# Per-graph products on 64 rows of the array, in a four-layer graph network on Trainium2

## The chip, the cores and the metric

The kernel runs on one core of a Trainium2 chip. TensorE multiplies matrices and writes PSUM, VectorE, ScalarE and GpSimd (POOL in the profile) do the elementwise work, and SyncE issues the DMAs. The metric is the device time of one execution in microseconds: 2607.68 us before, the median of four runs from 2606.7 to 2608.82.

## The reference

128 graphs of 64 nodes go through four layers; a node has 512 features. `adj` holds one 64 x 64 matrix per graph. All arithmetic is f32. Every layer first takes h = relu(layernorm(x)) and adds its result to x.

```python
# layer 0: hypergraph convolution, twice, with H = (adj != 0)
h = relu(hypergraph_conv(h, adj, W1, b1)); h = layer_norm(h, gamma, beta)
x = x + hypergraph_conv(h, adj, W2, b2) + h_in
# hypergraph_conv: D^-1 H B^-1 H^T (x W^T) + b, per graph
# layer 1: A = exp(lrelu(tanh(s_i + s_j))) * adj, normalised to P;  x = x + P h w
# layer 2: attention inside a graph, weight = adj * exp(q k^T), rows normalised
# layer 3: T = adj * exp(lrelu(s_i + s_j)), rows normalised
H = h Wk[0] + (T h) Wk[1] + (T T h) Wk[2] + biases;  x = x + relu(H)
```

Matrices that mix nodes (M = H B^-1 H^T of layer 0, P of layer 1, T and T² of layer 3) are 64 x 64 per graph. They are applied to h before the products with the weights.

## The kernel before

Two graphs share one tile of 128 rows (128 partitions), so x is 64 tiles of 128 x 512, worked on in 16 groups of four tiles. The mixing matrices of a tile's two graphs stand as a block-diagonal 128 x 128 matrix in a slot of the tag `bd`, whose off-diagonal blocks were set to zero once at the start; the two constants `HALVES` are the row ranges 0 to 63 and 64 to 127. Layers 0 and 1 are done for all groups, x goes out to DRAM and, after new weights have been loaded, layers 2 and 3 are done for all groups.

Products with weights use a Strassen scheme of seven products for a 2 x 2 block of tiles (`strassen`, `seven`; line 555 issues the matmuls, line 547 the sums on VectorE that it needs of its input). Ahead of them stand the products the change is about:

- `left_mul_T` computes (M h)^T in layer 0 and (P h)^T in layer 1 for a tile: four matmuls at line 502, each with 128 columns of h as weights and the block-diagonal matrix as 128 moving columns, into one PSUM bank; ScalarE copies the bank to SBUF at line 504, into a slot of `mT`. There are 128 such calls.
- In `layer3`, `tt` holds T^T and (T²)^T of a tile side by side, 256 columns. For each tile two operations `lm` at line 880 have two matmuls of 256 moving columns each, each operation with its own bank, and line 883 copies each bank into the tile's `a3`. Line 871 transposes h into the same `a3`.

The order of the instructions is neither the program's nor the hardware's choice. Every operation is recorded with an engine, an estimated cost, its reads and its writes (`pe`, `act`, `dve`, `pool`, `dma`); `Graph.run` then plans it all by list scheduling: on each engine the operation that could start first by these costs, ties by a priority that `step` moves on. A `Buf` gets a slot of its tag (a bank, for the tag `ps` with its eight banks) when its first operation is planned, and gives it back after its last. So a changed cost or a changed need for slots can move instructions on every queue, the DMA issues on SyncE's too. The cost of a group of matmuls is

```python
def c_mm(n, count):
    return 2 * count * max(n * 2 / 2400 + 0.0025, 0.111)
```

with n moving columns. Lines 413, 417 and 418 (`setup_l0`) are a few small matmuls near the start, the first with two columns of weights, the others with two rows.

Of the kernel before, what the change touches and what calls it, by code (L numbers as in the profile page):

```python
# [13 lines left out]
P = 128  # L14
C = 64
# [3 lines left out]
KD = D // P  # L19
# [19 lines left out]
class Graph:  # L39
# [41 lines left out]
    def run(self, slots, after):  # L81


        free = {tag: [(0.0, i) for i in range(len(ts))] for tag, ts in slots.items()}
        place = {}
        uses = dict.fromkeys(slots, 0)
        for o in self.ops:
            for b in o.bufs:
                uses[b.tag] += 1
        heirs = {}  # L90
        for tag, olds in after.items():
            for old in olds:
                heirs.setdefault(old, []).append(tag)
        waits = {tag: {old for old in olds if uses[old]} for tag, olds in after.items()}
        later = {tag: free[tag] for tag in after}
        for tag in after:
            free[tag] = []
        open_ = {e: [] for e in self.ENGINES}
        at = dict.fromkeys(self.ENGINES, 0.0)
        for o in self.ops:  # L100
            if not o.npre:
                open_[o.eng].append(o)
        order, left = [], len(self.ops)
        while left:
            best = None
            for e in self.ENGINES:

                t0, pick = None, None
                for o in open_[e]:
                    t = max(o.ready, at[e])  # L110
                    for b in o.bufs:
                        if id(b) not in place:
                            f = free[b.tag]
                            t = max(t, min(f)[0]) if f else float("inf")
                    if t0 is None or (t, o.prio, o.seq) < (t0, pick.prio, pick.seq):
                        t0, pick = t, o
                if pick is not None and (best is None or (t0, pick.prio) < (best[0], best[1].prio)):
                    best = t0, pick
            assert best and best[0] < float("inf"), "no operation can go on: too few slots"
            t, o = best  # L120
            open_[o.eng].remove(o)
            for b in o.bufs:
                if id(b) not in place:
                    s = min(free[b.tag])
                    free[b.tag].remove(s)
                    place[id(b)] = s[1]
                    b.t = slots[b.tag][s[1]]
            at[o.eng] = t + o.cost
            end = t + o.cost + self.LATENCY[o.eng]
            for b in o.bufs:  # L130
                b.users -= 1
                uses[b.tag] -= 1
                if not b.users:
                    free[b.tag].append((end, place[id(b)]))
                if not uses[b.tag]:
                    for tag in heirs.get(b.tag, ()):
                        waits[tag].discard(b.tag)
                        later[tag] = [(max(u, end), i) for u, i in later[tag]]
                        if not waits[tag]:
                            free[tag] = later[tag]  # L140
            for q in o.succ:
                q.npre -= 1
                q.ready = max(q.ready, end if q.eng != o.eng else t + o.cost)
                if not q.npre:
                    open_[q.eng].append(q)
            order.append((t, o.seq, o))
            left -= 1
        order.sort(key=lambda x: x[:2])
        for _, _, o in order:
            o.fn()  # L150
        return max(at.values()), {e: sum(o.cost for o in self.ops if o.eng == e) for e in self.ENGINES}
# [3 lines left out]
def tile_adj_preln_d4(  # L155
# [104 lines left out]
    def quad(b):  # L260
        return b.t.rearrange("p (c k) -> p c k", c=4)
# [233 lines left out]

    def left_mul_T(h, rhs, r, tag):

        p, m = Buf("ps"), Buf(tag)

        def mm():  # L500
            for c in range(KD):
                nc.tensor.matmul(quad(p)[:, c, :], h.t[:, c * P:(c + 1) * P], rhs(), start=True, stop=True)  # L502
        pe(c_mm(128, KD), mm, [h, *r], [p])
        act(0.59, lambda: nc.scalar.copy(m.t, quad(p)), [p], [m])  # L504
        return m

    def proj(lhsT, rhs, p, r, first=True, last=True):
# [110 lines left out]
    def layer0(g):  # L618
# [27 lines left out]
        for t0 in (0, 2):  # L646
# [12 lines left out]
            def emit_z(i, j, p, u, v, t0=t0, zs=zs):  # L659
# [1 line left out]
                scaled(lambda: z.t[:, cols], (z, j), lambda: rd.t[:, t:t + 1], [rd], lambda: b1_b[j].t, [b1_b[j]], p, u, v, D)  # L661
                act(0.63, lambda: nc.scalar.activation(z.t[:, cols], z.t[:, cols], AF.Relu), [(z, j)], [(z, j)])

            strassen(lambda i, j, mh=mh: mh[i].t[:, 2 * j:2 * j + 2, :], {(i, j): [mh[i]] for i in range(2) for j in range(2)},
                     W1, 2, D, "s1", emit_z)
            for i in range(2):
                z, rT = zs[i], rTs[i]
# [24 lines left out]
    def layer1(g):  # L692
        ad = adjs[g]
        hs, sg = [], Buf("col")
        for t in range(T):
            h = pre_ln(g, t)
            dot(lambda h=h: h.t, lambda: wa_b.t, lambda t=t: sg.t[:, t:t + 1], [h, wa_b], [(sg, t)])
            hs.append(h)
        z = bcast_sum(lambda: sg.t, lambda: sg.t, [(sg, t) for t in range(T)])
        act(0.42, lambda: nc.scalar.activation(z.t, z.t, AF.Tanh, scale=0.125), [z], [z])  # L700
        lrelu(z, 0.1)
        act(0.42, lambda: nc.scalar.activation(z.t, z.t, AF.Exp, scale=8.0), [z], [z])

        PT, pd, rn = Buf("bd"), Buf("ps"), Buf("ee")
        dve(0.42, lambda: nc.vector.tensor_mul(z.t, z.t, ad.t[:, 1]), [z, ad], [z])

        def sums():
            for i, m in enumerate((lambda: z.t, lambda: ad.t[:, 1])):
                nc.tensor.matmul(pd.t[:, i * T * C:(i + 1) * T * C], ones_bd, m().rearrange("p t c -> p (t c)"), start=True, stop=True)  # L709
        pe(c_mm(256, 2), sums, [z, ad], [pd])  # L710
        half = lambda i: pd.t[:, i * T * C:(i + 1) * T * C].rearrange("p (t c) -> p t c", t=T)
        dve(2.0, lambda: nc.vector.reciprocal(rn.t, half(0)), [pd], [rn])
        dve(0.42, lambda: nc.vector.tensor_mul(rn.t, rn.t, half(1)), [pd, rn], [rn])
        for s in HALVES:
            dve(0.42, lambda s=s: nc.vector.tensor_mul(PT.t[s, :, s], z.t[s], rn.t[s]), [z, rn], [(PT, s.start)])
        PTk = [(PT, 0), (PT, C)]
        step(1.0)
        for t0 in (0, 2):
            ph = [left_mul_T(hs[t], lambda t=t: PT.t[:, t, :], PTk, "mT") for t in (t0, t0 + 1)]
            step(1.8)  # L720

            def emit_w(i, j, p, u, v, t0=t0):
                xx, cols = xt[g, t0 + i], slice(j * D // 2, (j + 1) * D // 2)
                if u is not None:
                    U, iu = u
                    pool(0.75, lambda: nc.gpsimd.tensor_add(xx.t[:, cols], xx.t[:, cols], U.t[:, iu]), [xx, u], [xx])  # L726
                dve(c_v(D // 2), lambda: nc.vector.tensor_add(xx.t[:, cols], p.t[:, :D // 2], xx.t[:, cols]), [p, xx], [xx])

            strassen(lambda i, j, ph=ph: ph[i].t[:, 2 * j:2 * j + 2, :], {(i, j): [ph[i]] for i in range(2) for j in range(2)},
                     W, 2, D // 2, "s1", emit_w)  # L730
            for t in (t0, t0 + 1):
                xx = xt[g, t]
                xmid[g, t] = dram.tile([P, D], F32, name=f"xm{g}_{t}")
                dma(256, lambda xx=xx, t=t: nc.sync.dma_start(xmid[g, t], xx.t), [xx], [("xmid", g, t)])
# [96 lines left out]
    def layer3(g):  # L831
# [33 lines left out]
        for t0 in (0, 2):  # L865
            for t in (t0, t0 + 1):
# [4 lines left out]
                        nc.tensor.transpose(quad(p)[:, c, :], h.t[:, c * P:(c + 1) * P], ident)  # L871
                pe(KD * TR, tr0, [h], [p])
                act(0.59, lambda p=p, b=b: nc.scalar.copy(b.t[:, :KD, :], quad(p)), [p], [(b, 0)])
                for q in range(2):
                    pq = Buf("ps")

                    def lm(h=h, pq=pq, t=t, q=q):
                        for c in range(2):
                            cc = 2 * q + c
                            nc.tensor.matmul(pq.t[:, c * 2 * P:(c + 1) * 2 * P], h.t[:, cc * P:(cc + 1) * P],  # L880
                                             tt.t[:, t].rearrange("p j k -> p (j k)"), start=True, stop=True)
                    pe(c_mm(256, 2), lm, [h, (tt, 0), (tt, 1)], [pq])
                    act(0.59, lambda pq=pq, b=b, q=q: nc.scalar.copy(
                        b.t[:, KD:, :].rearrange("p (j c) k -> p c j k", j=2)[:, 2 * q:2 * q + 2],
                        pq.t.rearrange("p (c j k) -> p c j k", c=2, j=2)), [pq], [(b, 1 + q)])
                    step(0.9)
                step(0.45)

            def emit_o(i, j, p, u, v, t0=t0, os=[Buf("o"), Buf("o")]):
# [7 lines left out]
            ak = {}  # L897
            for i in range(2):
                b = a3[t0 + i]
                ak[i, 0] = [(b, 0), (b, 1)]  # L900
                ak[i, 1] = [(b, 1), (b, 2)]
            strassen(lambda i, j, t0=t0: a3[t0 + i].t[:, 6 * j:6 * j + 6, :], ak, W3, 6, D // 2, "s3", emit_o)

# [102 lines left out]
```

## Time and profile before

| | |
|---|---|
| profiled execution | 2606.7 us, span 2604.9 us |
| median of four runs | 2607.68 us |
| TensorE matmul | busy 2560.1 us, 12058 instructions |
| TensorE weight loads | busy 2046.2 us |
| VectorE | busy 1771.4 us |
| ScalarE | busy 783.2 us |
| GpSimd | busy 710.8 us |
| line 502 (M h, P h) | 1024 matmul records, all before 1320 us |
| line 880 (T, T²) | 512 matmul records, all after 1320 us |
| TensorE clock granted | 0.996 on average |

A matmul of f32 operands is two weight loads (PEld) and two matmul records (PE). The profile's time of one record is from its start until its results are out, and records overlap, so busy times of PE say little of how much more it could do; the step from record to record says more. Line numbers are those of the kernel before; in the kernel after, line 502 is 507, line 880 is 886 and line 555 is 561.

### The profile page before, as it was taken

Reading aid. Unit: us, or ns where it says so; the run is one execution under the profiler, and the core shown is the slowest. Engines: PE = TensorE matmul, PEld = TensorE weight load, DVE = VectorE, ACT = ScalarE, POOL = GpSimd, SP = SyncE. Lnnn points to the kernel's source line nnn. Section 1 sums busy time; section 2 is a strip of 40 time slices with the busy share of each in tenths; the row PEclk is TensorE's granted clock in tenths of the full one; section 3 lists DMA queues with packets and bytes.
Section 4 is the critical chain, followed back from the end, with each engine's and each line's share of the span. In section 5 each row is a group of like instructions: output and inputs, shape, how many; then the busy total and the mean of one; then the engine's idle time right before and its main releaser. Section 6 shows DMA issues by size and latency. Waiting matters only on the chain.

```text
span 2604.9 us, 32072 instructions
## 1 busy us (share of the span) xinstructions
PE 2560.1 (98%) x12058; PEld 2046.2 (79%) x12058; DVE 1771.4 (68%) x4064; ACT 783.2 (30%) x1370; POOL 710.8 (27%) x843
## 2 busy tenths in 40 slices
PE   8999999999999999999879999999999999999999
PEld 4767777777777777767768888888888888888887
DVE  8887788788787888778675545556456564555653
ACT  2343333343333433433222212222122221222211
POOL 3322334333233433333211212122221122211220
PEclk9999999999999999999989999999999999999999
DMA  4031001111001111101120110100101000010000
GB/s 166 17 110 37 20 22 37 33 37 37 21 21 37 33 37 37 37 10 32 65 89 21 33 33 25 37 25 29 33 24 37 29 29 33 21 37 25 25 21 25
DMA packets 53355, 96.18 MB, mean 37 GB/s; under 512 B 7760, under 2 KB 7760, under 8 KB 53200
## 3 DMA queue, kind: packets, MB, share of 16 engines
q1 hardware_dynamic: 53200, 94.14, 11.1%
q8 instruction: 94, 1.54, 0.3%
q14 instruction: 61, 0.50, 0.1%
HBM read 59.52 MB, written 34.60 MB: 36 GB/s over the span
## 4 chain that ended last, share of the span: by engine, by line
PE 95%; DVE 4%; issue 0%; ACT 0%; POOL 0%; DVEq 0%; ACTq 0%; POOLq 0%
PE ps L555 58%; PE ps L773 15%; PE ps L880 4%; PE ps L502 4%; PE ps L826 2%; PE ps L796 2%; PE ps L687 2%; PE ps L675 2%; PE ps L745 1%; PE ps L871 1%; DVE st L482 1%; DVE s_s_vu_tt L547 1%; PE ps L861 1%; PE ps L709 1%; PE ps L446 1%; PE ps L592 1%
## 5 line engine op out<-in xcount | busy, mean ns | idle before, releaser
L555 PE MATMUL ps<-wb_mem,rT_a 128*128 128x256 f32 x2056 | 476.2, 379 | 1.4 <-DVE u L527 0.8
L485 POOL TENSOR_TENSOR rs<-ve,mhalf 128x1 f32<-128x1 f32 x320 | 208.1, 653 | 935.7 <-DVE ve L484 874.0
L555 PEld LDWEIGHTS ps<-wb_mem,rT_a 128*128 128x128 f32 x2056 | 385.5, 190 | 67.2 <-issue 11.2
L493 ACT ACTIVATE h<-x,nm,rs 128x512 f32<-128x512 f32 x256 | 206.6, 815 | 360.3 <-DVE nm L492 270.9
L555 PE MATMUL ps<-wb_mem,s_s_vu_tt 128*128 128x256 f32 x1152 | 276.4, 379 | 0.1
L555 PE MATMUL ps<-wb_mem,tmp_s 128*128 128x256 f32 x1152 | 263.9, 379 | 0.0
L555 PEld LDWEIGHTS ps<-wb_mem,s_s_vu_tt 128*128 128x128 f32 x1152 | 215.6, 190 | 40.7 <-issue 7.3
L555 PE MATMUL ps<-wb_mem,mT_a 128*128 128x256 f32 x1016 | 243.3, 380 | 0.0
L555 PE MATMUL ps<-wa_mem,mT_a 128*128 128x512 f32 x512 | 240.1, 593 | 0.0
L555 PEld LDWEIGHTS ps<-wb_mem,tmp_s 128*128 128x128 f32 x1152 | 215.6, 190 | 27.5
L482 DVE BATCH_NORM_STATS2 st<-x 128x6 f32<-128x512 f32 x256 | 174.4, 686 | 63.4 <-DMA x<-xm 62.0
L555 PEld LDWEIGHTS ps<-wb_mem,mT_a 128*128 128x128 f32 x1016 | 190.5, 191 | 34.2 <-issue 7.7
L583 POOL TENSOR_TENSOR u<-u,bk_b 128x256 f32<-128x256 f32 x96 | 68.3, 726 | 472.0 <-DVE u L525 346.6
L555 PE MATMUL ps<-wa_mem,s_s_vu_tt 128*128 128x512 f32 x384 | 178.3, 594 | 5.5 <-DVE s_s_vu_tt L547 5.5
L527 DVE TENSOR_TENSOR u<-ps,u 128x512 f32<-128x512 f32 (+1 forms) x160 | 84.7, 529 | 115.6 <-PE ps L555 90.5
L555 PEld LDWEIGHTS ps<-wa_mem,mT_a 128*128 128x128 f32 x512 | 95.4, 190 | 85.7 <-issue 82.0
L502 PEld LDWEIGHTS ps<-bd,h 128*128 128x128 f32 x1024 | 131.1, 196 | 32.7 <-issue 18.7
L585 DVE TENSOR_TENSOR o<-ps,u 128x256 f32<-128x256 f32 x96 | 40.7, 424 | 153.5 <-PE ps L555 149.7
L504 ACT COPY mT_a<-ps 128x512 f32<-128x512 f32 x128 | 74.7, 584 | 233.6 <-PE ps L502 161.4
L726 POOL TENSOR_TENSOR x<-x,u 128x256 f32<-128x256 f32 x96 | 70.0, 742 | 260.8 <-DVE u L525 197.4
L502 PE MATMUL ps<-bd,h 128*128 128x128 f32 x1024 | 134.1, 280 | 6.9 <-ACT h L493 4.3
L555 PEld LDWEIGHTS ps<-wa_mem,s_s_vu_tt 128*128 128x128 f32 x384 | 71.9, 190 | 86.1 <-issue 68.6
(185 smaller groups left out, 4302.1 us busy)
## 6 DMA issues: line engine op xcount, KB each, us to landing
x<-in_x_dram SPq DMA_DIRECT2D x64, 256.0 KB, 2.8
xm<-x SPq DMA_DIRECT2D x64, 256.0 KB, 2.0
x<-xm SPq DMA_DIRECT2D x64, 256.0 KB, 2.6
out_dram<-x SPq DMA_DIRECT2D x64, 256.0 KB, 2.0
adj<-in_adj_dram SPq DMA_DIRECT2D x32, 256.0 KB, 2.6
wb_mem<-in_Wk_dram SPq DMA_DIRECT2D x6, 512.0 KB, 7.6
wa_mem<-in_W1T_dram SPq DMA_DIRECT2D x2, 1024.0 KB, 7.7
wb_mem<-in_W2T_dram SPq DMA_DIRECT2D x4, 512.0 KB, 6.4
```

The costliest lines, as they stand in the source:

```text
L482: dve(0.69, lambda i=i: nc.vector.bn_stats(st.t[:, i, :], src(i)), [r[i]], [(st, i)])
L485: pool(0.57, lambda: nc.gpsimd.tensor_tensor(rs.t, ve.t, mhalf, ALU.pow), [ve], [rs])
L493: act(0.82, lambda: nc.scalar.activation(h.t, xx.t, AF.Relu, bias=nm.t, scale=rs.t), [xx, nm, rs], [h])
L502: nc.tensor.matmul(quad(p)[:, c, :], h.t[:, c * P:(c + 1) * P], rhs(), start=True, stop=True)
L504: act(0.59, lambda: nc.scalar.copy(m.t, quad(p)), [p], [m])
L527: dve(c_v(n), lambda: nc.vector.tensor_add(at(2)(), p4.t[:, :n], at(1)()), [p4, (U, 1)], [(U, 2)])
L555: nc.tensor.matmul(p.t[:, :n], lhs()[:, c, :], rhs(c), start=first and c == 0, stop=c == kc - 1, skip_group_check=True)
L583: pool(0.75, lambda: nc.gpsimd.tensor_add(U.t[:, iv], U.t[:, iu], row()[:, cols]), [u, krow], [v])
L675: nc.tensor.transpose(quad(pt)[:, c, :], z.t[:, j * D + c * P:j * D + (c + 1) * P], ident)
L726: pool(0.75, lambda: nc.gpsimd.tensor_add(xx.t[:, cols], xx.t[:, cols], U.t[:, iu]), [xx, u], [xx])
L773: nc.tensor.matmul(pair(p.t)[:, o, :], a, b, start=first and o == 0 and c == 0, stop=c == 1, skip_group_check=True)
L880: nc.tensor.matmul(pq.t[:, c * 2 * P:(c + 1) * 2 * P], h.t[:, cc * P:(cc + 1) * P], tt.t[:, t].rearrange("p j k -> p (j k)"), start=True, ...
```

## The change

Each of the two products is split by graph: one matmul takes the 64 rows of the first graph and its 64 x 64 block, another the 64 rows of the second. The two go by turns and write two PSUM banks, one per graph. In `left_mul_T` a matmul has 64 moving columns; a call has eight instead of four, and two ScalarE copies of 256 columns instead of one of 512. In `layer3`, the four matmuls of 256 columns of a tile become eight of 128, in one operation instead of two, with two copies of 512 columns as before, now by graph and not by column. The zero blocks are no longer multiplied. The planner learns to wait until as many slots of a tag are free as an operation needs, and the costs and the keys of reads and writes follow.

```diff
@@ Graph.run
+                    need = {}
                     for b in o.bufs:
                         if id(b) not in place:
-                            f = free[b.tag]
-                            t = max(t, min(f)[0]) if f else float("inf")
+                            need[b.tag] = need.get(b.tag, 0) + 1
+                    for tag, n in need.items():
+                        f = free[tag]
+                        t = max(t, (min(f) if n == 1 else sorted(f)[n - 1])[0] if len(f) >= n else float("inf"))
@@ left_mul_T
-        p, m = Buf("ps"), Buf(tag)
+        p, m = [Buf("ps"), Buf("ps")], Buf(tag)
         def mm():
             for c in range(KD):
-                nc.tensor.matmul(quad(p)[:, c, :], h.t[:, c * P:(c + 1) * P], rhs(), start=True, stop=True)
-        pe(c_mm(128, KD), mm, [h, *r], [p])
-        act(0.59, lambda: nc.scalar.copy(m.t, quad(p)), [p], [m])
+                for i, half in enumerate(HALVES):
+                    nc.tensor.matmul(p[i].t[:, c * C:(c + 1) * C], h.t[half, c * P:(c + 1) * P], rhs()[half, half], start=True, stop=True)
+        pe(c_mm(64, KD), mm, [h, *r], p)
+        for i, half in enumerate(HALVES):
+            act(0.38, lambda i=i, half=half: nc.scalar.copy(m.t[:, :, half], p[i].t[:, :KD * C].rearrange("p (c k) -> p c k", c=KD)), [p[i]], [(m, i)])
@@ layer0 and layer1, keys of the Strassen products' input
-            {(i, j): [mh[i]] for i in range(2) for j in range(2)}
+            {(i, j): [(mh[i], 0), (mh[i], 1)] for i in range(2) for j in range(2)}
@@ layer3
-                for q in range(2):
-                    pq = Buf("ps")
-                    def lm(h=h, pq=pq, t=t, q=q):
-                        for c in range(2):
-                            cc = 2 * q + c
-                            nc.tensor.matmul(pq.t[:, c * 2 * P:(c + 1) * 2 * P], h.t[:, cc * P:(cc + 1) * P],
-                                             tt.t[:, t].rearrange("p j k -> p (j k)"), start=True, stop=True)
-                    pe(c_mm(256, 2), lm, [h, (tt, 0), (tt, 1)], [pq])
-                    act(0.59, lambda pq=pq, b=b, q=q: nc.scalar.copy(
-                        b.t[:, KD:, :].rearrange("p (j c) k -> p c j k", j=2)[:, 2 * q:2 * q + 2],
-                        pq.t.rearrange("p (c j k) -> p c j k", c=2, j=2)), [pq], [(b, 1 + q)])
-                    step(0.9)
+                pq = [Buf("ps"), Buf("ps")]
+                def lm(h=h, pq=pq, t=t):
+                    for c in range(KD):
+                        for i, half in enumerate(HALVES):
+                            nc.tensor.matmul(quad(pq[i])[:, c, :], h.t[half, c * P:(c + 1) * P], tt.t[half, t, :, half],
+                                             start=True, stop=True)
+                pe(c_mm(128, KD), lm, [h, (tt, 0), (tt, 1)], pq)
+                for i, half in enumerate(HALVES):
+                    act(0.59, lambda pq=pq, b=b, i=i, half=half: nc.scalar.copy(
+                        b.t[:, KD:, half].rearrange("p (j c) k -> p c j k", j=2),
+                        pq[i].t.rearrange("p (c j k) -> p c j k", c=KD, j=2)), [pq[i]], [(b, 1 + i)])
+                step(0.9)
                 step(0.45)
...
-                ak[i, 0] = [(b, 0), (b, 1)]
+                ak[i, 0] = [(b, 0), (b, 1), (b, 2)]
```

More of the change, by code (lines that the diff above doesn't have):

```diff
@@ L662, in emit_z @@
                 act(0.63, lambda: nc.scalar.activation(z.t[:, cols], z.t[:, cols], AF.Relu), [(z, j)], [(z, j)])
-            strassen(lambda i, j, mh=mh: mh[i].t[:, 2 * j:2 * j + 2, :], {(i, j): [mh[i]] for i in range(2) for j in range(2)},
+            strassen(lambda i, j, mh=mh: mh[i].t[:, 2 * j:2 * j + 2, :], {(i, j): [(mh[i], 0), (mh[i], 1)] for i in range(2) for j in range(2)},
                      W1, 2, D, "s1", emit_z)
@@ L727, in emit_w @@
                 dve(c_v(D // 2), lambda: nc.vector.tensor_add(xx.t[:, cols], p.t[:, :D // 2], xx.t[:, cols]), [p, xx], [xx])
-            strassen(lambda i, j, ph=ph: ph[i].t[:, 2 * j:2 * j + 2, :], {(i, j): [ph[i]] for i in range(2) for j in range(2)},
+            strassen(lambda i, j, ph=ph: ph[i].t[:, 2 * j:2 * j + 2, :], {(i, j): [(ph[i], 0), (ph[i], 1)] for i in range(2) for j in range(2)},
                      W, 2, D // 2, "s1", emit_w)
```

## The prediction

> **What bounds the kernel now.** I read the page's busy times and its chain first, then the groups split by shape, then the timeline at the lines the change touches. The page:
>
> ```profile
> PE 2560.1 (98%) x12058; PEld 2046.2 (79%) x12058; DVE 1771.4 (68%) x4064; ACT 783.2 (30%) x1370; POOL 710.8 (27%) x843
> ...
> PE 95%; DVE 4%; issue 0%; ACT 0%; POOL 0%; DVEq 0%; ACTq 0%; POOLq 0%
> ```
>
> TensorE is the chain: what its instruction stream gets longer or shorter, the span does, unless another engine has no room. The groups by shape:
>
> ```profile
> L502 PE MATMUL ps<-bd,h 128*128 128x128 f32 x1024 | 134.1, 280 | 6.9 <-ACT h L493 4.3 <-DVE bd L715 2.4
> L504 ACT COPY mT_a<-ps 128x512 f32<-128x512 f32 x128 | 74.7, 584 | 233.6 <-PE ps L502 161.4 <-PE ps L555 58.7 <-DVE s_s_vu_tt L547 13.5
> L880 PE MATMUL ps<-s_s_vu_tt,h 128*128 128x256 f32 x512 | 120.5, 379 | 0.0
> L523 ACT COPY u<-ps 128x256 f32<-128x256 f32 x96 | 35.7, 372 | 103.4 <-PE ps L555 103.4
> ```
>
> Each f32 matmul of the program leaves two records, so line 502 has 512 matmuls (128 calls of four), line 880 has 256 (64 tiles of four). The mean of one (280, 379 ns) is a latency; what a stream costs is the step from record to record, which the timeline gives:
>
> ```profile
> 46.65 0.97 PEld L635 LDWEIGHTS ps<-mB,bd 128*128 128x128 f32 x8
> 1000.47 2.75 PEld L502 LDWEIGHTS ps<-bd,h 128*128 128x128 f32 x24 [0.58 <-DVE bd L715]
> 1513.08 3.62 PE L880 MATMUL ps<-s_s_vu_tt,h 128*128 128x256 f32 x16
> ```
>
> A line's length less one record's own, over the records but one: (2.75 - 0.19)/23 = 0.111 us at line 502 with 128 moving columns, (0.97 - 0.19)/7 = 0.111 at line 635 with 65. So at and below 128 columns the step doesn't follow the columns: a weight load of 128 columns sets it. At 256 columns the matmul sets it: (3.62 - 0.38)/15 = 0.216.
>
> The changed matmuls use 64 rows of the array. The trace has only four places where the part of the array in use changes: into and out of line 413 (two columns of weights) and lines 417 and 418 (two rows).
>
> ```profile
> 34.55 1.45 PE L555 MATMUL ps<-wa_mem,s_s_vu_tt 128*128 128x512 f32 x3
> 35.93 1.02 PE L413 MATMUL ps<-wb_mem,gsc 128*2 128x512 f32 x2
> ...
> 41.94 1.02 PE L413 MATMUL ps<-wb_mem,gsc 128*2 128x512 f32 x2
> 42.89 0.44 PE L675 MATMUL ps<-ident,z_hT 128*128 128x128 f32 x2
> ...
> 43.93 0.49 PE L675 MATMUL ps<-ident,z_hT 128*128 128x128 f32 x3
> 44.35 1.12 PE L417 MATMUL ps<-o,tmp_s 2*128 2x512 f32 x2
> ...
> 45.31 1.02 PE L418 MATMUL ps<-o,tmp_s 2*128 2x512 f32 x2
> 46.26 0.55 PE L675 MATMUL ps<-ident,z_hT 128*128 128x128 f32 x3
> ```
>
> Records of 512 columns step by 0.43. The last L413 began at 41.94 + 0.43 = 42.37, would let the next start at 42.80, and that starts at 42.89: 0.09 late. The other three come out at 0.09 too (35.84 to 35.93; 44.26 to 44.35, with transposes stepping 0.109; 46.17 to 46.26, where ScalarE's h also ends just then). At an ordinary border, L502 to L555, there is no such hole. Besides, the next load is not under way: the L417 pair takes 1.12 where 0.43 + 0.59 = 1.02 would do (0.10 more), the L675 pair 0.44 for 0.38 (0.06 more). One change of shape costs 0.15 to 0.19 us.
>
> **The change part by part.**
>
> *Products with T and T² (line 880 before).* Removed: per tile eight records at 0.216, 1.73 us, 110.6 over 64 tiles. Added: per tile eight matmuls, 16 records of 128 moving columns on 64 rows, two row groups by turns. If the groups work side by side, each has eight loads at 0.111: 0.89 per tile, a gain of 0.84 each, 53.7 in all. If no two loads overlap, 16 x 0.111 = 1.78, a loss of 0.05 each, 3 in all. No row shows two row groups at once; these are the ends. I take the first.
>
> *M h and P h (line 502 before).* Removed: eight records at 0.111, 0.89 per call, 114 over 128 calls. Added: 16 records of 64 columns. Line 635 says that fewer columns don't shorten the step, so side by side it is 0.89 again, gain 0; one at a time 1.78, a loss of 0.89 each, 114 in all. I take 0. In these groups nothing is to be won even at best.
>
> [...]
>
> *Borders between the shapes.* In the changed kernel's instruction order the 64-row matmuls stand in 122 unbroken runs: 88 in layers 0 and 1 (65 of one call, 6 of two, 17 of three), 34 in layer 3 (19 of one tile, 15 of three). A run pays 0.19 on entry (0.09 and 0.10, as at L417) and 0.15 to 0.19 on leaving; mostly an f32 product follows, whose load is like L417's, so 0.19: 0.38 x 122 = 46.4. [...] And in each run the second row group ends about one load after the first, since a matmul's two records stand together and its group's turn comes after: 0.11 x 122 = 13.4; ends 0 and 13.4.
>
> *ScalarE copies.* Line 504's one copy of 584 ns becomes two of 256 columns, nearest row L523 at 372: +0.16 a call, 20 us on an engine that is busy 783. Cost nothing: it hides in ScalarE's idle time, and what waits for it, the sums of line 547 on VectorE, waited 13.4 us for mT_a in the whole run. On the path each time, it would be 20. Line 883's two copies per tile keep their size, but the first starts only after the whole product, some 0.9 later at most; the sums of layer 3 now wait for all three pieces. VectorE is at 726 of 1295 us in the second half (windows view), so 0 there too; were each of the 64 tiles 0.9 late on the path, 58.
>
> *PSUM.* A call holds two of eight banks instead of one, for 0.37 longer. What TensorE now waits for a bank's readers is 1.4 us (L555 on VectorE's u). I take 0, with an upper end of 10.
>
> *The plan.* Costs and needs in the planner change, so every queue is reordered: SP's 324 rows become 326, POOL's 677 become 676, with the loads and the inputs of POOL's adds moved along. TensorE's waits in the list of waits add up to 40 us (9.9 for ScalarE's h at the turn to layer 2, 6.1 at the start). I take them unchanged; a plan may move them 10 either way.
>
> Sum: -53.7 + 46.4 + 13.4 = +6.1. The profiled execution took 2606.7, the median is 2607.7: **2613**.
>
> **Rivals.**
>
> *Shape changes are free (the other side).* Place: the 122 runs. Then -53.7 + 13.4 = -40: 2566. The sign turns at (53.7 - 13.4)/122 = 0.33 us per run, entry and exit together. [...] Against it: four of four show the 0.09, among them both directions.
>
> *Records go out strictly in order.* [...] If a row group's load may not pass the other group's waiting record, then per four records (two of one group, two of the other) only a matmul and the other group's first load overlap: three steps of 0.11 at 64 columns, 1.31 per call of M h, and four at 128, 1.78. That is 128 x 0.42 + 64 x 0.05 + 46.4 = +103: 2710. [...]
>
> *Loads one at a time.* 114 + 3 + 46.4 = +163: 2770. The same comes if a record can't follow another in under 0.056 us, the pace of line 635 (two records per 0.111): 32 records a call are 1.78. For it: the load's 0.111 is the rigid number of this trace. Against it: at 42.89 a load and its matmul start together, so records can follow faster.
>
> **How the numbers follow.** Side by side with paid borders 0.50: 2613, own range 2595 (exit 0.15, no trailing group) to 2630 (PSUM and plan against it). In order 0.22: 2710. One at a time 0.18: 2770. Free borders 0.10: 2566. Faster and slower count from 0.2%, about 5 us, which is what a measurement here can tell. Faster: 0.10 and a quarter of the first, 0.23; same: a quarter of the first, 0.12; slower the rest, 0.65. The range reaches from 2592 to 2780; it leaves out the free borders and a little above.
>
> **What would show it.** Right: records of line 507 and 886 starting in pairs, one per row group, 0.11 per pair; a hole of 0.09 before and after each run; line 886's stretch per tile near 1.0 and not 1.73; ScalarE at some 803; TensorE's waits near 40. Wrong on the side of loss: 16 steps of 0.11 per call, the first half of the span longer by over 100. Wrong on the side of gain: no holes. The forecast falls if the pairs overlap only in part, since the gain and the price of the borders nearly cancel.

## The result, and the profile after

The changed kernel takes 2610.55 us (median of 41 runs, 2608.8 to 2613.6) against 2606.91 before (61 runs, 2605.94 to 2608.87; the 2607.68 above was the median of four): ratio 1.0014, 95% interval 1.001 to 1.0018. That is 3.6 us slower, clear of the noise but inside the 0.2% that the prediction counts as no change, and it hides a loss and a gain of some 30 us each. The profiled execution took 2610.86 us (before: 2606.7) with a span of 2609.0.

The page after the change, its busy times and its chain:

```profile
PE 2557.4 (98%) x13594; PEld 2015.9 (77%) x13594; DVE 1790.3 (69%) x4064; ACT 790.3 (30%) x1498; POOL 707.6 (27%) x843
...
PE 94%; DVE 5%; ACT 1%; issue 1%; POOL 0%; DVEq 0%; ACTq 0%; POOLq 0%
```

TensorE is still the chain, with 1,536 matmul records more. The groups by shape that answer to lines 502, 504 and 880:

```profile
L507 PE MATMUL ps<-bd,h 64*128 64x64 f32 x2048 | 137.7, 280 | 6.2 <-ACT h L496 4.2 <-DVE bd L721 2.0
L510 ACT COPY mT_a<-ps 128x256 f32<-128x256 f32 x256 | 81.7, 374 | 193.5 <-PE ps L507 121.2 <-PE ps L561 62.7 <-DVE s_s_vu_tt L553 9.3
L886 PE MATMUL ps<-s_s_vu_tt,h 64*128 64x128 f32 x1024 | 66.8, 279 | 9.5 <-ACT s_s_vu_tt L869 9.5
```

The matmuls of M h and P h doubled in number and kept their busy time (134.1 before, 137.7 now); those of T and T² doubled too, and theirs fell from 120.5 to 66.8. The 9.5 us of idle time before line 886 is new: line 880 had 0.0. The timeline of the kernel after, first TensorE's matmuls at three calls of line 507 in a row, then its weight loads there, then one tile of line 886 in the same two views; the line at the head is of the kernel before, three calls of line 502:

```profile
1000.55 2.87 PE L502 MATMUL ps<-bd,h 128*128 128x128 f32 x24
...
1009.60 0.59 PE L693 MATMUL ps<-y_qT,bd 128*128 128x512 f32 x1
1010.12 2.90 PE L507 MATMUL ps<-bd,h 64*128 64x64 f32 x48
1013.38 0.70 PE L561 MATMUL ps<-wa_mem,mT_a 128*128 128x512 f32 x1 [0.36 <-ACT mT_a L510]
...
1010.12 2.76 PEld L507 LDWEIGHTS ps<-bd,h 64*128 64x128 f32 x48 [0.76 <-issue]
...
1590.56 1.16 PE L886 MATMUL ps<-s_s_vu_tt,h 64*128 64x128 f32 x16
1591.65 3.70 PE L832 MATMUL ps<-s_s_vu_tt,bd 128*128 128x512 f32 x8
...
1590.55 0.97 PEld L886 LDWEIGHTS ps<-s_s_vu_tt,h 64*128 64x128 f32 x16
```

Three calls of line 507 have 48 records in the 2.9 us that 24 records of line 502 took before. Two loads, one per row group, go out per step, and the two of a pair start 0.007 us apart (in 1,398 of the 1,536 pairs). From the first of 24 pairs to the last there are 23 steps, from the first of eight to the last there are seven: (2.76 - 0.19 - 0.007)/23 = 0.111 us a pair at line 507 and (0.97 - 0.19 - 0.007)/7 = 0.110 at line 886. A single record of line 880 took 0.216. So the step of a pair is that of one record on all 128 rows (0.111 at line 502), at 64 moving columns and at 128. And the hole at the border is there: the last record of L693 began at 1009.60, its 512 columns take 0.43, and the next starts at 1010.12 and not at 1010.03, 0.09 late, as at lines 413 and 417 before.

The list of TensorE's waits after:

```profile
PE ps L877 <- ACT h L496: 9.9, 1, 9.9
PE ps L886 <- ACT s_s_vu_tt L869: 9.5, 14, 0.7
PE ps L641 <- DVE mB L636: 6.1, 1, 6.1
PE ps L598 <- DVE dg L596: 4.5, 1, 4.5
PE ps L507 <- ACT h L496: 4.2, 3, 3.7
PE ps L561 <- ACT mT_a L510: 2.1, 6, 0.4
```

Two lines are new: 9.5 us for the copy of T² (14 times 0.7) and 2.1 for the two copies of mT, one of which stands in the timeline above. Another line shrank, TensorE's wait for the sums of VectorE, first before and then after:

```profile
PE ps L555 <- DVE s_s_vu_tt L547: 5.5, 7, 1.0
...
PE ps L561 <- DVE s_s_vu_tt L553: 0.8, 1, 0.8
```

All of TensorE's waits in the list come to 39.9 us before and 46.4 after.

The turn from the first two layers to the last two shows in the end of M h and P h: their last record ended at 1316.9 us before and ends at 1349.5 now, 32.6 later, while what follows it went from 1288.0 to 1259.5, 28.5 less.

### The profile page after: what moved, and what is told of

The parts are those of the page before. It is cut to its first block, busy times and chain, and to the rows that moved or that the text cites. A ratio compares the mean times of both kernels' runs of the same rounds, so it can differ in the third digit from the quotient of the medians.

```text
span 2609.0 us, 35323 instructions
## 1 busy us (share of the span) xinstructions
PE 2557.4 (98%) x13594; PEld 2015.9 (77%) x13594; DVE 1790.3 (69%) x4064; ACT 790.3 (30%) x1498; POOL 707.6 (27%) x843
## 4 chain that ended last, share of the span: by engine, by line
PE 94%; DVE 5%; ACT 1%; issue 1%; POOL 0%; DVEq 0%; ACTq 0%; POOLq 0%
PE ps L561 58%; PE ps L779 15%; PE ps L507 4%; PE ps L886 3%; PE ps L832 2%; PE ps L681 2%; PE ps L802 2%; PE ps L693 2%; PE ps L751 1%; PE ps L877 1%; DVE u L579 1%; DVE st L485 1%; PE ps L867 1%; PE ps L598 1%; PE ps L715 1%
## 5 line engine op out<-in xcount | busy, mean ns | idle before, releaser
L488 POOL TENSOR_TENSOR rs<-ve,mhalf 128x1 f32<-128x1 f32 x320 | 197.6, 620 | 1133.0 <-DVE ve L487 1120.0
L561 PE MATMUL ps<-wb_mem,s_s_vu_tt 128*128 128x256 f32 x1152 | 282.9, 384 | 0.9 <-DVE s_s_vu_tt L553 0.8
L507 PEld LDWEIGHTS ps<-bd,h 64*128 64x128 f32 x2048 | 124.9, 191 | 51.0 <-issue 24.9
L529 ACT COPY u<-ps 128x512 f32<-128x512 f32 (+1 forms) x160 | 73.3, 458 | 242.4 <-PE ps L561 141.8
L507 PE MATMUL ps<-bd,h 64*128 64x64 f32 x2048 | 137.7, 280 | 6.2 <-ACT h L496 4.2
L510 ACT COPY mT_a<-ps 128x256 f32<-128x256 f32 x256 | 81.7, 374 | 193.5 <-PE ps L507 121.2
L589 POOL TENSOR_TENSOR u<-u,bk_b 128x256 f32<-128x256 f32 x96 | 81.4, 867 | 207.5 <-DVE u L533 100.7
L668 ACT ACTIVATE z_hT<-z_hT 128x512 f32<-128x512 f32 x128 | 80.8, 633 | 179.3 <-DVE z_hT L581 177.2
```

Source lines behind the costliest of these rows:

```text
L488: pool(0.57, lambda: nc.gpsimd.tensor_tensor(rs.t, ve.t, mhalf, ALU.pow), [ve], [rs])
L507: nc.tensor.matmul(p[i].t[:, c * C:(c + 1) * C], h.t[half, c * P:(c + 1) * P], rhs()[half, half], start=True, stop=True)
L510: act(0.38, lambda i=i, half=half: nc.scalar.copy(m.t[:, :, half], p[i].t[:, :KD * C].rearrange("p (c k) -> p c k", c=KD)), [p[i]], [(m, i)])
L529: act(n / 1200 + 0.17, lambda: nc.scalar.copy(at(0)(), p1.t[:, :n]), [p1], [(U, 0)])
L561: nc.tensor.matmul(p.t[:, :n], lhs()[:, c, :], rhs(c), start=first and c == 0, stop=c == kc - 1, skip_group_check=True)
L589: pool(0.75, lambda: nc.gpsimd.tensor_add(U.t[:, iv], U.t[:, iu], row()[:, cols]), [u, krow], [v])
```

## The experiments

### Each half of the change alone

The first version takes over the change of `layer3` and leaves `left_mul_T`; the second the reverse.

The main lines of the first edit, shortened (the copies, the costs and the keys go back with them):

```diff
 # t_only: left_mul_T as before
-        for c in range(KD):
-            for i, half in enumerate(HALVES):
-                nc.tensor.matmul(p[i]..., h.t[half, ...], rhs()[half, half], ...)
+        for c in range(KD):
+            nc.tensor.matmul(quad(p)[:, c, :], h.t[:, c * P:(c + 1) * P], rhs(), start=True, stop=True)
 ...
 # mp_only: layer3 as before, two operations lm of two matmuls of 256 columns
```

> Only the products with T and T^2 are split by graph; M h and P h stay as before. Theory (row groups work side by side, every run of 64-row matmuls pays for its two borders): 34 runs in layer 3 instead of 122. Line by line from the timelines of the two kernels, the stretches of these products with their borders and the new wait for tt add up to 30 us less than before: 2577, ratio 0.988. Rival (the parts are each near zero, the small result hides no gain and no loss): 2604 to 2610. Rival (waits and the new plan ate the gain of layer 3): no better than 2600, and a longer list of TensorE's waits.

> Only M h and P h are split by graph; layer 3 stays as before. Theory: 88 runs in layers 0 and 1, each 0.34 us longer than the full-height call that it replaces, nothing won inside: 2607 + 30 to 32 = 2638, ratio 1.012. Rival (each part near zero): 2604 to 2610. Rival (ScalarE's second copy or the second bank is what costs): longer too, but with holes at line 561 for mT_a or for VectorE's u and none at the borders.

T and T² alone: 2577.4 us (4 runs), ratio 0.9887, interval 0.987 to 0.9903: 29 less than the 2606.5 beside it. M h and P h alone: 2641.1 (4 runs), ratio 1.0129, interval 1.0114 to 1.0144: 35 more. Expected were 2577 and 2638. The sum of the two, +5.5, is near the whole change's +3.6. So the near zero is a gain and a loss that cancel, and the rival of two parts near zero falls. In the first version the wait for tt stands as in the kernel after:

```profile
PE ps L883 <- ACT s_s_vu_tt L866: 9.4, 14, 0.7
```

In the second, the waits for mT come to 2.2 us, which leaves the greater part of the 35 to the borders: a run of a single call (there are 65) takes 1.24 us from the end of the work ahead to the start of the work behind, with the weight load behind it that nothing hides, and a single call on full height takes 0.90 (medians). The 0.34 between them times 88 runs is 30.

### The price of a border by itself

```diff
         def mm():
+            nc.tensor.matmul(quad(p)[:, 0, :C], h.t[:C, :P], rhs()[:C, :C], start=True, stop=True)   # extra64
+            nc.tensor.matmul(quad(p)[:, 0, :C], h.t[:, :P], rhs()[:, :C], start=True, stop=True)     # extra128
             for c in range(KD):
```

> The kernel before, with one more matmul at the head of each of the 128 calls for M h and P h: 64 rows, 128 columns of weights, 64 moving columns, its result overwritten by the call's own first matmul; the plan is the same as before. Theory (a change of shape costs 0.2 us each way): per call 0.20 + 0.11 + 0.05 + 0.20 = 0.56, in all +72: 2679. Rival (changes of shape are free): as the 128-row control, +28: 2635.

> The control: the same additional matmul on all 128 rows, so two more records and no change of shape. Both theories: 2 x 0.111 x 128 = +28: 2635. The difference to the 64-row version is the price of 128 pairs of borders: 43 us by the theory (0.34 each), 0 by the rival.

2673.6 us (3 runs) and 2630.0 (3 runs), ratios 1.0257 (1.024 to 1.0274) and 1.0094 (1.0077 to 1.0111). Both are some 5 us under what was expected, as the control's two records cost 23.5 us and not 28. The difference of the two is 43.6 us, 0.34 per pair of borders, where 43 was expected. The timelines of TensorE in the two, at one call each:

```profile
1033.44 1.02 PE L688 MATMUL ps<-y_qT,bd 128*128 128x512 f32 x2
1034.40 0.43 PE L501 MATMUL ps<-bd,h 64*128 64x64 f32 x2
1034.76 1.16 PE L503 MATMUL ps<-bd,h 128*128 128x128 f32 x8
```

```profile
1019.73 0.33 PE L501 MATMUL ps<-bd,h 128*128 128x64 f32 x2
1019.90 1.11 PE L503 MATMUL ps<-bd,h 128*128 128x128 f32 x8
```

From the start of the additional matmul to the start of the call proper it is 0.36 us with a change of shape and 0.17 without; ahead of the 64 rows another 0.09 goes (1033.44 + 2 x 0.43 = 1034.30, the start is 1034.40; unrounded 0.092), and the call's first weight load is no longer hidden (1.16 for 1.11). The rival of free borders falls.

### How far ahead the other row group may start

The same matmuls and the same plan, but in another order inside a product: four of the first graph and then four of the second; two and two; three, three, one and one. The kernel after takes turns of one.

```diff
-            for c in range(KD):
-                for i, half in enumerate(HALVES):
+            for i, half in enumerate(HALVES):          # by_graph
+                for c in range(KD):
+            for i, c in ((0, 0), (0, 1), (1, 0), (1, 1), (0, 2), (0, 3), (1, 2), (1, 3)):   # by_two
+            for i, c in ((0, 0), (0, 1), (0, 2), (1, 0), (1, 1), (1, 2), (0, 3), (1, 3)):   # by_three
```

> The kernel after, with the two loops inside each product swapped: all four matmuls of the first graph, then all four of the second, where they went by turns. Same matmuls, banks, borders and plan. Theory (records for another row group can start while earlier records of the first still wait, as far ahead as the hardware looks): if it looks at least 8 matmul records ahead, no change, 2608 to 2613. Rival (records go out strictly in order, and only neighbours overlap): the two graphs run one after the other, 1.78 instead of 0.89 a call, 192 x 0.85 = +163: 2774. In between: a look-ahead of a few records.

> The kernel after, with the matmuls of each product in turns of two (two of the first graph, two of the second, and so on: 4 records a turn). In the version graph by graph, the second graph's first load began when the fifth of eight records had begun, that is, with three matmul records of the first still waiting. Theory (up to three matmul records of a row group may wait without holding up what comes behind): with four records to a turn the second group starts at once, no change: 2609 to 2613. Rival (each turn of a group has to end before the other starts, or the overlap is a fixed share of a turn): half way to the version graph by graph, 2640 to 2650.

> As before in turns of three, then one of each (6 records, 6 records, 2, 2). Theory (three may wait): the second group starts when the third record of the first has begun, some 0.27 us late, once per call and not once per run, and later turns catch up in part: 192 x 0.2 to 0.27 = +38 to +52 at most, less where calls stand together and the lag is already there; 2630 to 2660. If it comes out at 2611, more than three may wait.

| matmul records to a turn | time, us | ratio (interval) | a run of a single call is longer by (line 507 / line 886), us |
|---|---|---|---|
| 2 (the kernel after) | 2610.6 | 1.0014 (1.001 to 1.0018) | 0 / 0 |
| 4 | 2617.2 | 1.0037 (1.0024 to 1.0051) | 0.05 / 0.10 |
| 6 | 2643.7 | 1.0139 (1.0119 to 1.0159) | 0.27 / 0.32 |
| 8 | 2686.4 | 1.0302 (1.0282 to 1.0322) | 0.49 / 0.55 |

A turn is what one row group issues before the other is up. The last column, the lag, compares a run of a single call, or tile, with that of the kernel after. Neither end came: with eight records to a turn the groups overlap in part. Three tiles of line 886 in a row show it, in this version and then in the kernel after:

```profile
1516.61 3.93 PE L886 MATMUL ps<-s_s_vu_tt,h 64*128 64x128 f32 x48
```

```profile
1545.98 2.99 PE L886 MATMUL ps<-s_s_vu_tt,h 64*128 64x128 f32 x48 [0.68 <-ACT s_s_vu_tt L869]
```

In the trace the first group's fifth matmul record begins at 1517.159, and the second group's first load at 1517.164: three records of the first group still wait then. All 19 runs of a single tile show the same, and in the version of six the second group's first load comes just after the third record of six has begun, again with three waiting. With four records to a turn, where three wait behind the first, the second group starts at once, 0.007 us after the first. That turn costs a lag of 0.05 to 0.10 even so: 2617.2 lies 4 us above the expected 2609 to 2613. From there each two records more to a turn cost 0.22 us, two steps. For six I had expected a lag in every call; it comes once per run (0.27 in the runs of one call and in those of three), so 122 x 0.27 = 33, and 33 were measured. So in these runs records did hold up what stood behind them, but only from the fourth that waited (0.27 to 0.55 us in turns of six and eight). And matmuls of one group passed those of the other: the second group's first record begins at 1517.165, the first group's last, which stands ahead of it in the program, at 1517.494. The version with eight has one more thing against it: its granted clock was 0.992 on average in the profiled execution and 0.991 in the other two, against 0.995 in the kernel after. The reason is not shown.

### The new wait for T²

The planner puts the products with T and T² right behind the one that makes T², and TensorE waits for ScalarE's copy. A greater estimated cost for that copy lets the planner put two transposes of h between them; what is computed stays.

```diff
-        act(0.59, lambda: nc.scalar.copy(tt.t[:, :, 1, :], quad(p2)), [p2], [(tt, 1)])
+        act(1.40, lambda: nc.scalar.copy(tt.t[:, :, 1, :], quad(p2)), [p2], [(tt, 1)])
```

> As the version with only T and T^2 by graph, but the planner is told 1.40 instead of 0.59 us for ScalarE's copy of T^2 (tt), so that in 15 of 16 groups two transposes of h (line 874, 2 x 0.44 us) come between the product that makes T^2 and the first product that uses it. Nothing is computed differently. Theory (the 9.4 us that TensorE waits at line 883 for that copy, 14 times 0.7, is a wait of the plan, with work at hand to fill it): 2577.4 - 9 = 2568, and the wait is gone from the list. Rival (the wait moves to another place, as ScalarE or a bank is late): 2575 to 2580, with a new line in the list of waits.

> The same planner cost in the kernel after. Theory: 2610.6 - 9 = 2601, ratio 0.998 to the kernel before, so that without this one wait the whole change would have come out a little faster. Rival: 2608 to 2612, nothing gained.

With T and T² alone: 2568.3 us (4 runs), ratio 0.9851, interval 0.9837 to 0.9864. With the whole change: 2601.2 (11 runs), ratio 0.9979, interval 0.997 to 0.9988. Both are 9 less than without the edit, and the wait is gone from the list (the first version):

```profile
PE ps L874 <- ACT h L496: 9.9, 1, 9.9
PE ps L638 <- DVE mB L633: 6.1, 1, 6.1
PE ps L558 <- DVE s_s_vu_tt L550: 5.5, 7, 1.0
PE ps L505 <- ACT h L496: 4.5, 3, 3.7
```

The first of the two is the fastest kernel here: 38 us under the kernel before.

## Why the prediction was right, point by point

The predicted 2613 us stand against 2610.6, and the case named likeliest, side by side with paid borders, is the one that holds. The gain and the price of the borders were right in their sizes. Two other terms, the trailing group and the waits, were wrong by some 12 us each, and it is luck that they offset each other. By its own measure of 5 us the prediction gave "slower" 0.65 and "same", where 3.6 us falls, 0.12.

- **Gain at T and T²: right.** Predicted 0.111 per step of two loads and 53.7 us in all; measured 0.110 to 0.112, so 64 x (1.73 - 8 x 0.111) = 54.
- **No gain at M h and P h: right.** 0.111 a pair, as a record before; the half alone shows a loss only.
- **Price of the borders: right in sum.** Predicted 0.19 each way, 46.4 in all. In M h a run pays 0.09 ahead of its first pair, 0.05 until its second pair (0.16 us instead of 0.11), 0.10 ahead of the work behind and 0.10 for the load there: 0.34, times 88 runs 30. The 34 runs of T and T² take 81.2 us; less 64 x 0.89 for their steps and 9.5 for the wait, 15 are left, 0.43 a run. Together 45.
- **The trailing group, 13.4: wrong.** I had taken a matmul's two records to keep the other group waiting for a step. The two groups' records start 0.007 apart: 0.9 in all, which the 45 hold. The orders of six and eight show that a lag of that kind comes only when more than three records wait.
- **Waits unchanged: wrong.** The plan brought 9.5 for the copy of T², and ScalarE's second copy of mT 2.1, 11.6 together. I had set the copies at nothing because VectorE hardly waited for mT; it was TensorE that came to wait, where three calls stand together (the line at 1013.38). The other waits became 5 us shorter, so that the list grew by 6.5, within the 10 that the prediction allowed the plan.
- **ScalarE's time: over-sized, without effect.** Predicted 20 us more, measured 7.1 (783.2 to 790.3): of two copies in a row, part overlaps, as 256 copies of 374 ns are busy for 81.7 us.
- **The clock** was left out of the sum. At the turn of the layers the trace has the clock at half for 20 us in the kernel before and for 27 in the kernel after. TensorE is idle there for 22 and for 18 us. The windows view over 160 us at that place, before and after (behind the window stand its length and TensorE's busy time; the clock is the third number from the end):

```profile
1240.00:1400.00 160.00, 138.23 (x669) 116.07 (x667) 97.02 (x205) 38.24 (x67) 34.46 (x43) 0.94 0.19 61
```

```profile
1270.00:1430.00 160.00, 141.76 (x746) 119.11 (x745) 97.33 (x211) 38.46 (x73) 35.77 (x45) 0.91 0.16 53
```

  Seven more at half are at most 3.4 us. How much of it they cost is not shown; the half with M h and P h alone has it (0.91), and the other has not (0.94). Single runs show that a thousandth of granted clock goes with some 2 us: the kernel before took 2606.5 us in 18 of the runs beside the experiments, with a clock of 0.996, and 2608.5 in 16 with 0.995 (medians); the kernel after took 2610.2 in 33 runs with 0.995 and 2612.4 in nine with 0.994. At 0.995 the two are 1.7 us apart.

The new sum is -54 + 45 + 11.6 = +3; measured +3.6 in the medians and +4.2 in the profiled executions. The timelines say the same without the terms. Line 886's 34 runs take 81.2 us, borders and waits included, where line 880 took 110.4; line 507's 88 runs take 158.8, where line 502 took 126.6. That is +3.0 of the 4.1 us by which the span grew. The last 1.1 is a balance that the runs do not tell apart: other waits became 5 us shorter, and the longer stretch at half clock and the rest of the new plan took that back.

The rivals: free borders fall by the pair with one additional matmul; loads one at a time fall by the 0.111 per pair; strict order falls by the 0.007 between the groups and by the matmul that passes three others. The faster side had 0.23, and one moved operation would have put the change there: 2601.2.

## What to carry to other kernels

Splitting a block-diagonal product by row groups paid here where a record of 256 moving columns stepped by 0.216 us (a pair of 128 columns each took 0.111) and not where one of 128 columns already stepped by 0.111 (a pair of 64 columns each took 0.111 too): look at the step from record to record before halving the columns. Count the unbroken runs, as each cost 0.34 to 0.43 us here, and let the groups take turns that are as short as possible: two records cost nothing here, four 7 us in all. And when a planner orders the work, read the list of waits after every change of an operation's length: 9 of the 39 us that T and T² could give went into one wait that two transposes at hand would fill.

## What the runs showed of the hardware

- Two row groups of 64 loaded weights at the same time: 16 loads of 128 columns took 0.97 us (line 886), and eight loads on all 128 rows took as long (line 635 before).
- A change between 128 and 64 rows cost 0.09 us of standing still and, in part or in full, a weight load that nothing hides: 0.14 (line 507) to 0.19 (line 886) on the way in and 0.20 on the way out. The turns between the two 64-row groups cost no such hole: the two loads of a pair mostly start 0.007 us apart, and inside a run pairs mostly follow each other every 0.110 to 0.112.
- Up to three matmul records of one row group waited without holding up the other group's start; beyond that each cost a step of 0.11 us (at line 886 the second group's first load starts 0.01 us after the first group's in turns of four records, 0.33 in turns of six, 0.55 in turns of eight). In turns of eight, matmuls of the second group started ahead of matmuls of the first that stand before them in the program (1517.165 against 1517.494).
